# A stacked graph kernel: the first pair of batches split into two halves, and PSUM banks given out as asked for

## The chip, the cores and the metric

The kernel runs on one core of one Trainium2 chip. The time is the device time of one execution in microseconds (us), the median of several runs. A profiled execution is one more run, with every instruction recorded. The engines are named PE (TensorE matmul), PEld (TensorE weight load, which overlaps PE), DVE (VectorE), ACT (ScalarE), POOL (GpSimd) and SP (SyncE, which issues transfers here).

## The reference, cut to what matters

The input x has 64 batches of 256 nodes with 128 features, in float32; adj is a 256x256 matrix shared by all batches. Four layers follow one another, each on a layer norm with a ReLU and each added to x:

```python
h = relu(layernorm(x)); x = x + gated(h, adj)     # five recurrent steps, each: m = adj @ h for each batch,
                                                  # r, z = sigmoid gates of m and h, hv = tanh(W5 m + U5 (r*h)),
                                                  # h = (1 - z) * h + z * hv
h = relu(layernorm(x)); x = x + relu([h, A'h, A'A'h ...] @ Theta + bias)
h = relu(layernorm(x)); y = (adj @ h + h) @ W + bias; x = x + y / max(norm(y), 1e-12)
h = relu(layernorm(x))
pre[b,i,j,:] = W1 h[b,i] + W2 h[b,j] + b_lin      # 256 features for each of 256 x 256 pairs of nodes
e[b,i,j] = sum over features of a * leaky_relu(pre) + adj[i,j]
x = x + sigmoid(softmax_j(e) @ h)
```

The last layer's scores e are most of the work: 64 x 256 x 256 pairs of nodes with 256 features each.

## The kernel before

**Tiling.** The 64 batches are taken two at a time: 32 pairs, and a feature-by-node tile of a pair is 128 partitions x 512 columns (2 batches x 256 nodes). For each pair, `front(p)` computes the first three layers and the operands of the scores; then 64 slots of score work follow, 32 for each of two blocks of 128 rows i (`ic`); then `tail(p, ic, ...)` makes the softmax and the output of one block.

**A front.** It is a Python generator that yields where it must wait: `yield ENGINE, since, bank, gate`. A recurrent step is a chain over engines: PE mixes nodes (`mix_nodes`), ACT copies the result out (mT), PE projects (u3t, w4t), ACT takes the tanh for r, DVE makes rh, PE projects (w34, w5t, u5t), ACT takes two tanhs, three elementwise passes follow on DVE (for pairs after the first, one of them, d, is on POOL), PE turns the result to token order (`to_token`) and ACT copies it out (h). After the fifth step come x1, a norm, two mixes and three products (x2), a norm, a mix, a product and a norm of rows (x3), a last norm, and four projections: s2a and s2c, s2n, s1b, s1a. A small matmul, `quarter`, and a trip through DRAM (`row`, `rows`) give two more operands that only a tail reads.

**A score tile.** A slot n stands for four rows i (32 apart) of both batches, and has two halves (k = 0 and 1) of 128 features. One tile is 128 x 4 x 2 x 256. `work_on_tile` makes it: DVE with one instruction (k = 0, from s1a and s2a in PSUM), ACT with 16 small ones (k = 1, from s1b and s2p in PSUM), POOL with 8 small ones (either). For three slots in ten, POOL issues a DMA that adds one half onto the other (`add_pair`). `score` then lets PE sum over features with four matmuls of 512 columns into the block's bank. 13 buffers (`tiles`) hold score tiles.

**Order.** There is no scheduler at run time. A planner in the program keeps a clock for each engine with estimated durations, and always lets the engine that is least far choose: tails first, then fronts in the order of their keys (constants for the first pairs are chains too, keys -1 and NPAIR), then score tiles. `in_order` fixes each engine's program to the order in which it was chosen. At the beginning the fronts of pairs 0 and 1 are begun together; one more is begun for each pair scored. A front p with 0 < p < NPAIR is held to a due time while a bank is spare (`chain_ready`: `due = STEPS_OF_FRONT * (scored / 128 - (p - 2)) / SPREAD`, with SPREAD 1.7). The constants must be complete ("all" in `SET_UP`) before a front may start its second layer.

**PSUM.** Eight tiles of 128x512, `banks`, are dealt out by hand: two for s2a (`s2v`, by the parity of p), one for s2p, two for the scores (`pes`, by the parity of the block), and three in a list `spare` that fronts and tails take from and give back to. While no score is made yet, pair 0's front uses the banks of s2p and the scores for its r, pr and pv.

```python
s2v = banks[:2]
s2p = banks[2].rearrange("p (b n) -> p b n", b=NB)
pes = banks[3:5]
...
spare = [[b, 0.0] for b in banks[5:]]
```

Of the kernel before, what the change touches and what calls it, by code (L numbers as in the profile page):

```python
# [31 lines left out]
def kernel(  # L32
# [63 lines left out]
    s2v = banks[:2]  # L96
    s2p = banks[2].rearrange("p (b n) -> p b n", b=NB)
    pes = banks[3:5]
# [19 lines left out]
    spare = [[b, 0.0] for b in banks[5:]]  # L118
# [6 lines left out]
    def by_feature(b):  # L125
        return b.rearrange("p (b n) -> p b n", b=NB)

    def by_token(b):
        return b.rearrange("p (b c n) -> p b c n", b=NB, c=NC)
# [262 lines left out]
    def inverse_root(t, of, *scaled):  # L392

        nc.gpsimd.tensor_scalar(t, of, scaled[0], scaled[2], op0=scaled[1], op1=scaled[3])
        nc.gpsimd.tensor_tensor(t, t, minus_half, op=OP.pow)  # L395
# [9 lines left out]
    def project(pp, w, t, start=True, stop=True):  # L405

        side_by_side(pp, w, flat(t), start, stop)

    def mix_nodes(pm, h, a):

        pm = by_feature(pm)
        for b in range(NB):
            for c in range(NC):
                side_by_side(pm[:, b, :], h[:, b, c, :], a[:, c, :], c == 0, c == NC - 1)

    def to_feature(pt, h):

        pt = by_token(pt)
        for b in range(NB):
            for c in range(NC):  # L420
                nc.tensor.transpose(pt[:, b, c, :], h[:, b, c, 0:D], ident)

    def to_token(pt, ht):

        pt = by_token(pt)
        for b in range(NB):
            for c in range(NC):
                nc.tensor.transpose(pt[:, b, c, :], ht[:, b, c * P:(c + 1) * P], ident)  # L428

    def project_token(pp, pairs):  # L430

        pp = by_token(pp)
        for b in range(NB):
# [16 lines left out]
    PROJECT, MIX, TURN, PRODUCT, PRODUCTS = 0.86, 1.74, 0.80, 0.88, 2.64  # L450
    COPY, BIASED, TANH, ELEMENTS = 0.48, 0.58, 0.57, 0.61

    def norm(src, since, h):

        stats = work.tile([P, NB * NC, 3], F32, name="stats")
        mv = work.tile([P, NB * NC, 2], F32, name="mv")
        s, h = rows_of(src), rows_of(h)[:, :, 0:D]
        yield DVE, since
        for k in range(0, NB * NC, 2):
            nc.vector.bn_stats(stats[:, k:k + 2, :].rearrange("p k s -> p (k s)"), s[:, k:k + 2, :].rearrange("p k d -> p d k"))  # L460
        t = ran(DVE, 0.8, since)
# [7 lines left out]
        for k in range(NB * NC):  # L469
            nc.scalar.activation(h[:, k, :], s[:, k, :], AF.Relu, bias=mv[:, k, 0:1], scale=mv[:, k, 1:2])  # L470
        return ran(ACT, 1.55, t)

    def copied(name, bank, t):

        c = feat(name, **(SHORT if name not in KEPT else KEPT[name]))
        nc.scalar.copy(c, by_feature(bank[0]))  # L476
        t = ran(ACT, COPY, t)
        spare.append([bank[0], t])
        return c, t

    KEPT = {"hT": dict(bufs=4), "hT3": {}, "s2n": {}}

    READY = {}

    def front(p):
# [4 lines left out]
        x0 = XIN.pop(p)  # L490


        h = tok("h", **SHORT)
# [5 lines left out]
        t = ran(PE, TURN, t, b[1])  # L499
        yield ACT, t  # L500
        hT, t_hT = copied("hT", b, t)
        for step in range(STEPS):
# [3 lines left out]
            t = ran(PE, MIX, t_h, b[1])  # L506
            yield ACT, t
            mT, t_m = copied("mT", b, t)
            if p == 0:
                pr, r, pv = ([banks[k], 0.0] for k in (3, 2, 4))  # L510
                yield PE, t_hT, 0, lambda: "first" in SET_UP
                project(pr[0], u3t, hT, stop=False)
                ran(PE, PROJECT, t_hT)
                yield PE, t_m
                project(pr[0], w4t, mT, start=False)
                t = ran(PE, PROJECT, t_m)
                project(pv[0], w5t, mT, stop=False)
                ran(PE, PROJECT)
                yield ACT, t
            else:  # L520
# [4 lines left out]
                t = ran(PE, 2 * PROJECT, t_m, t_hT, pr[1])  # L525
                yield ACT, t, 1
                r = take()
            nc.scalar.activation(r[0], pr[0], AF.Tanh, bias=br, scale=0.5)  # L528
            t = ran(ACT, TANH, t, r[1])
            yield DVE, t  # L530
            rh = feat("rh", **SHORT)
            nc.vector.scalar_tensor_tensor(rh, by_feature(r[0]), 1.0, hT, op0=OP.add, op1=OP.mult)  # L532
            t_rh = ran(DVE, ELEMENTS, t)
            if p == 0:
                yield PE, t
                project(pr[0], w34, mT, start=False)
                t_z = ran(PE, PROJECT, t)
                yield PE, t_rh
                project(pv[0], u5t, rh, start=False)
                t = ran(PE, PROJECT, t_rh)  # L540
            else:
                spare.append([r[0], t_rh])
                yield PE, t_rh, 1
                project(pr[0], w34, mT, start=False)
                t_z = ran(PE, PROJECT, t)
# [3 lines left out]
                t = ran(PE, 2 * PROJECT, t_rh, pv[1])  # L549
            yield ACT, t_z  # L550
            nc.scalar.activation(pr[0], pr[0], AF.Tanh, bias=bz, scale=0.5)  # L551
            t_z = ran(ACT, TANH, t_z)
            yield ACT, t

            d = feat("d", **SHORT)
            if p < 1:
                nc.scalar.activation(pv[0], pv[0], AF.Tanh, bias=bh, scale=1.0)
                t = ran(ACT, TANH, t)
                yield DVE, t
                nc.vector.tensor_sub(d, by_feature(pv[0]), hT)  # L560
                t = ran(DVE, ELEMENTS, t)
            else:
                nc.scalar.activation(d, by_feature(pv[0]), AF.Tanh, bias=bh, scale=1.0)  # L563
                t = ran(ACT, TANH, t)
# [5 lines left out]
            nc.vector.scalar_tensor_tensor(by_feature(pr[0]), by_feature(pr[0]), 1.0, d, op0=OP.add, op1=OP.mult)  # L570
            t = ran(DVE, ELEMENTS, t, t_z)
            yield DVE, t
            hT_new = feat("hT", bufs=4)
            nc.vector.scalar_tensor_tensor(hT_new, by_feature(pr[0]), 0.5, hT, op0=OP.mult, op1=OP.add)  # L574
            hT = hT_new
            t_hT = ran(DVE, ELEMENTS)
            if p > 0:
                spare.append([pr[0], t_hT])
# [3 lines left out]
            t = ran(PE, TURN, t_hT, b[1])  # L582
            if step < STEPS - 1:
                yield ACT, t
                h = tok("h", **SHORT)
                nc.scalar.copy(h, by_token(b[0]))  # L586
                t_h = ran(ACT, COPY, t)
                spare.append([b[0], t_h])
        yield DVE, t
        x1 = tok("x1", tag="x12", bufs=3)  # L590
        nc.vector.tensor_add(x1, x0, by_token(b[0]))
        t = ran(DVE, ELEMENTS, t)
# [3 lines left out]
        h = tok("h", **SHORT)  # L596
# [4 lines left out]
        t = ran(PE, MIX, t_h, b[1])  # L601
# [5 lines left out]
        t = ran(PE, TURN, t_h, b[1])  # L607
        yield ACT, t
        hT, t = copied("hT", b, t)
# [3 lines left out]
        t = ran(PE, MIX, t_h, b[1])  # L613
# [5 lines left out]
        t = ran(PE, PRODUCTS, t, po[1])  # L619
        yield DVE, t  # L620
        pt = rows_of(by_token(po[0]))
        nc.vector.tensor_add(pt, pt, bias1.unsqueeze(1).to_broadcast([P, NB * NC, D]))
        t = ran(DVE, ELEMENTS, t)
        yield DVE, t
        x2 = tok("x2", tag="x12", bufs=3)
        nc.vector.scalar_tensor_tensor(x2, by_token(po[0]), 0.0, x1, op0=OP.max, op1=OP.add)
        t = ran(DVE, ELEMENTS)
# [3 lines left out]
        h = tok("h", **SHORT)  # L631
# [4 lines left out]
        t = ran(PE, MIX, t, b[1])  # L636
# [5 lines left out]
        t = ran(PE, PRODUCT, t, po[1])  # L642
        yield DVE, t
        pt = rows_of(by_token(po[0]))
        nc.vector.tensor_add(pt, pt, bias2.unsqueeze(1).to_broadcast([P, NB * NC, D]))
        t = ran(DVE, ELEMENTS, t)
        yield ACT, t
        sq = tok("sq", **SHORT)
        nc.scalar.square(sq, by_token(po[0]))
        t = ran(ACT, COPY, t)  # L650
        yield DVE, t
        rn = work.tile([P, NB * NC], F32, name="rn")
        nc.vector.tensor_reduce(rn, rows_of(sq), AX.X, OP.add)
        t = ran(DVE, ELEMENTS, t)
# [5 lines left out]
        x3 = tok("x3")  # L660
        for k in range(NB * NC):
            nc.vector.scalar_tensor_tensor(rows_of(x3)[:, k], pt[:, k], rn[:, k:k + 1], rows_of(x2)[:, k],
                                           op0=OP.mult, op1=OP.add)
        t = ran(DVE, 1.04, t)
# [3 lines left out]
        h3 = work.tile([P, NB, NC, D + 1], F32, name="h3")  # L668
# [5 lines left out]
        t = ran(PE, TURN, t, b[1])  # L674
        yield ACT, t
        hT, t_hT = copied("hT3", b, t)
        s2a = s2v[p % 2]
        yield PE, max(t_hT, t_s2v[p % 2])
        project(s2a, w2n[:, 0:P], hT)
        t_s2a = ran(PE, PROJECT, t_hT, t_s2v[p % 2])  # L680
        yield ACT, t_s2a
        s2c = feat("s2c")
        nc.scalar.copy(s2c, by_feature(s2a))
        t_s2a = ran(ACT, COPY, t_s2a)
        yield PE, t_hT, 1
        b = take()
        tokens = flat(hT).rearrange("p (q g i) -> p q g i", g=4, i=32)
        for g in range(4):
            nc.tensor.matmul(b[0][g * 32:(g + 1) * 32, 0:P], g2, tokens[:, :, g, :], start=True, stop=True, skip_group_check=True)
        t = ran(PE, 0.35, t_hT, b[1])  # L690
        yield ACT, t
        quarter = work.tile([P, P], F32, name="quarter", bufs=1)
        nc.scalar.copy(quarter, b[0][:, 0:P])
        t = ran(ACT, 0.3, t)
        spare.append([b[0], t])
        yield DVE, t
        turned = work.tile([P, P], F32, name="turned", bufs=1)
        nc.vector.transpose(turned, quarter)
        s1o = work.tile([P, NB * NC], F32, name="s1o")
        nc.vector.tensor_scalar(s1o, turned[:, 2:P:32], b_odd, None, op0=OP.add)  # L700
        ran(DVE, 0.4, t)
        row = dram.tile([2, NB * N], F32, name="row", bufs=2)
        for k in range(2):
            nc.sync.dma_start(row[k].rearrange("(q g i) -> g q i", g=4, i=32), quarter[k:P:32, :].rearrange("g (q i) -> g q i", i=32))
            t = moved(t) if k else max(t, moved(t) - 2.2)
        rows = work.tile([P, 2, NB, N], F32, name="rows")
        nc.sync.dma_start(rows.rearrange("p k b n -> p (k b n)"), row.rearrange("k t -> (k t)").unsqueeze(0).to_broadcast([P, 2 * NB * N]))
        lin, s2o = rows[:, 0], rows[:, 1]
# [5 lines left out]
        t = ran(PE, PROJECT, t_hT, b[1])  # L714
        yield ACT, t
        s2n, t_2 = copied("s2n", b, t)
# [343 lines left out]
```

## Time and profile before

| | |
|---|---|
| median of 3 runs | 4939.74 us (4939.73 to 4947.85) |
| the profiled execution | 4942.53 us, span of its instructions 4940.7 us |
| PE, DVE, ACT, POOL busy | 96%, 95%, 94%, 94% of the span |
| granted TensorE clock, mean | 0.995 of full |
| large score tiles | 1817 on DVE, 231 + 785 on POOL, 1263 on ACT |
| DMA adds of one half onto the other | 614, of 1024 KB each, 7.9 us to landing |

A line of the timeline gives the start and the duration in us, the engine, the line of the kernel, the operation, the tile written and the tiles read with their shapes, and how many in a row; in brackets, how long the engine was idle before and what released it. A line of the busy time by stretch gives the stretch, its length, then for PE, PEld, DVE, ACT and POOL the busy us and the number of instructions, then the granted clock, the busy share of the DMA engines and GB/s. A line of the waits gives who waited for whom, the us in total, how often, and the longest.

### The profile page before, as it was taken

The page shows a single profiled execution, that of the slowest core. Times are in us where ns is not written, and L with a number is a line of the kernel's source. Part 1 is how long each engine was busy: PE and PEld are TensorE (multiplying, and loading weights), DVE is VectorE, ACT ScalarE, POOL GpSimd, SP SyncE. Part 2 cuts the span into 40 slices and gives each one's busy share as a digit, 9 for nine tenths or more (in the row PEclk, how much of TensorE's full clock was granted, in tenths as well). Part 3 has the DMA queues.
Part 4 walks back from the last instruction along what each step waited for, and adds up shares of the span by engine and source line. Part 5 has one row for each costly group of instructions (what it writes and reads, how often), then busy time and mean ns, then how long its engine had stood idle before and what let it go on. Part 6 is the DMA issues. An engine that isn't in the chain of part 4 may idle for free. (4 is left out here: it accounts for less than half of the span.)

```text
span 4940.7 us, 133662 instructions
## 1 busy us (share of the span) xinstructions
PE 4758.5 (96%) x52231; PEld 1739.0 (35%) x52231; DVE 4682.1 (95%) x3358; ACT 4644.4 (94%) x12121; POOL 4659.6 (94%) x9446
## 2 busy tenths in 40 slices
PE   8999999999999999999999999999999999999987
PEld 3333333333333333333333333333334333333322
DVE  3999999999999999999999999999999999999998
ACT  3999999999999999999999999999999999999998
POOL 1999999999999999999999999999999999999998
PEclk9999999999999999999999999999999999999999
DMA  0577677677666676766677676767666766766677
GB/s 18 121 144 146 142 147 144 135 144 147 140 142 138 141 155 143 145 139 139 140 146 145 139 145 130 155 139 146 134 137 141 151 137 140 146 141 141 142 158 148
DMA packets 133132, 687.42 MB, mean 139 GB/s; under 512 B 15121, under 2 KB 49809, under 8 KB 53905
## 3 DMA queue, kind: packets, MB, share of 16 engines
q0 software_dynamic: 88416, 643.86, 65.1%
q1 hardware_dynamic: 43360, 35.01, 2.3%
q8 instruction: 408, 6.68, 0.5%
q14 instruction: 228, 1.86, 0.1%
q10 hardware_dynamic: 720, 0.00, 0.0%
HBM read 26.48 MB, written 8.52 MB: 7 GB/s over the span
## 5 line engine op out<-in xcount | busy, mean ns | idle before, releaser
L873 ACT ACTIVATE rl<-bank,s1b 128x256 f32<-128x256 f32 x10104 | 4050.2, 793 | 128.9 <-DMA rl<-rl 70.9
L859 DVE TENSOR_TENSOR rl<-s1a,bank 128x2048 f32<-128x2048 f32 x1817 | 4064.8, 2280 | 90.4 <-DMA rl<-rl 62.7
L881 POOL TENSOR_SCALAR rl<-s2n,s1b 128x256 f32<-128x256 f32 x6280 | 2951.1, 656 | 64.2 <-DMA rl<-rl 28.2
L940 PE MATMUL bank<-rl,win_n 128*32 128x512 f32 x17752 | 2191.5, 594 | 57.1 <-DVE rl L859 28.9
L940 PE MATMUL bank<-rl,win 128*32 128x512 f32 x10104 | 1316.5, 594 | 0.0
L940 PEld LDWEIGHTS bank<-rl,win_n 128*32 128x32 f32 x17752 | 559.4, 110 | 1216.5 <-issue 992.8
L881 POOL TENSOR_SCALAR rl<-s2c,s1a 128x256 f32<-128x256 f32 x1848 | 872.7, 637 | 5.9 <-DMA rl<-rl 1.2
L898 POOL DMA_DIRECT2D rl<-rl x614 | 569.9, 940 | 22.2 <-DVE rl L859 10.8
L940 PEld LDWEIGHTS bank<-rl,win 128*32 128x32 f32 x10104 | 323.1, 110 | 641.4 <-issue 533.1
L400 PE MATMUL bank<-mT,wts 128*32 128x512 f32 x2560 | 336.6, 597 | 6.5 <-ACT mT L476 4.9
L400 PE MATMUL bank<-adj_t,h 128*32 128x256 f32 x5120 | 310.6, 383 | 13.7 <-ACT h L586 13.4
L567 POOL TENSOR_TENSOR d<-d,hT 128x512 f32<-128x512 f32 x155 | 230.4, 1486 | 71.3 <-ACT d L563 71.2
L400 PEld LDWEIGHTS bank<-adj_t,h 128*32 128x32 f32 x5120 | 164.0, 111 | 191.2 <-issue 51.1
L470 ACT ACTIVATE h<-x,mv 128x128 f32<-128x128 f32 x384 | 177.7, 699 | 10.6 <-DVE mv L466 9.7
L428 PE MATMUL bank<-ident,hT 128*128 128x128 f32 x640 | 105.4, 288 | 69.2 <-DVE hT L574 61.7
L400 PE MATMUL bank<-hT,wts 128*32 128x512 f32 x1280 | 168.7, 597 | 0.0
L400 PE MATMUL bank<-mT,w 128*32 128x512 f32 x1280 | 167.4, 593 | 0.8 <-ACT bank L528 0.8
L400 PE MATMUL bank<-rh,u5t 128*32 128x512 f32 x1280 | 167.3, 592 | 0.7 <-DVE rh L532 0.7
L528 ACT ACTIVATE bank<-bank,gate_b 128x512 f32<-128x512 f32 x160 | 144.3, 902 | 20.5 <-PE bank L400 16.5
L476 ACT COPY mT<-bank 128x512 f32<-128x512 f32 x160 | 139.3, 871 | 24.1 <-PE bank L400 20.0
L551 ACT ACTIVATE bank<-bank,gate_b 128x512 f32<-128x512 f32 x160 | 151.4, 946 | 11.3 <-PE bank L400 11.3
L563 ACT ACTIVATE d<-bank,gate_b 128x512 f32<-128x512 f32 x155 | 150.0, 967 | 7.4 <-PE bank L400 7.4
(167 smaller groups left out, 3382.2 us busy)
## 6 DMA issues: line engine op xcount, KB each, us to landing
rl<-rl POOLq DMA_DIRECT2D x614, 1024.0 KB, 7.9
rows<-row SPq DMA_DIRECT2D x32, 512.0 KB
xin<-in_x_dram SPq DMA_DIRECT2D x64, 128.0 KB
out_dram<-o SPq DMA_DIRECT2D x64, 128.0 KB
row<-quarter SPq DMA_DIRECT2D x64, 2.0 KB
w_raw<-in_L_gnn_w_w_dram SPq DMA_DIRECT2D x3, 128.0 KB
th_raw<-in_L_gnn_Theta_dram SPq DMA_DIRECT2D x1, 320.0 KB
adj_n<-in_adj_dram SPq DMA_DIRECT2D x1, 256.0 KB
```

The source lines that it names most:

```text
L400: nc.tensor.matmul(o[g:g + 32], w[:, g:g + 32], t, start=start, stop=stop, skip_group_check=True)
L470: nc.scalar.activation(h[:, k, :], s[:, k, :], AF.Relu, bias=mv[:, k, 0:1], scale=mv[:, k, 1:2])
L476: nc.scalar.copy(c, by_feature(bank[0]))
L528: nc.scalar.activation(r[0], pr[0], AF.Tanh, bias=br, scale=0.5)
L551: nc.scalar.activation(pr[0], pr[0], AF.Tanh, bias=bz, scale=0.5)
L563: nc.scalar.activation(d, by_feature(pv[0]), AF.Tanh, bias=bh, scale=1.0)
L567: nc.gpsimd.tensor_sub(d, d, hT)
L859: nc.vector.tensor_tensor(t, rows.to_broadcast(whole), ops["s2a"].unsqueeze(1).to_broadcast(whole), op=OP.min)
L873: nc.scalar.activation(t[:, g, b, :], s2p[:, b, :], AF.Relu, bias=ops["s1"][1][:, b, i:i + 1], scale=-1.0)
L881: nc.gpsimd.tensor_scalar(t[:, part, b, :], ops["s2n" if k else "s2c"][:, b, :], ops["s1"][min(k, 1)][:, b, row], MOST_NEGATIVE, op0=OP.mi ...
L898: nc.gpsimd.dma_start(out=t.rearrange("p g b n -> p (g b n)"), in_=z.rearrange("p g b n -> p (g b n)"), accum_op=OP.add)
L940: nc.tensor.matmul(pe[g * 32:(g + 1) * 32, :], w[:, 31 - r:63 - r], flat(t[:, g]), start=False, stop=(left[block] == 0), skip_group_check= ...
```

## The change

The helpers of a front (`mix_nodes`, `to_feature`, `to_token`, `project_token`, `norm`) and the planner's estimates take the number of batches, one or two, instead of always two. `front(p, batches)` is begun twice for the first pair, with one batch each, under keys 0 and 0.5; both are `alone`. Such a front works on 256 columns; its tiles of the moment are pieces of two score tiles each (`lent`), which go back to `tiles` at its end, and its lasting tiles (`kept`) are halves of tiles shared by both. An `alone` front keeps the order of operations that pair 0 had, with d on DVE.

For the first pair a block of scores is now one batch with all its 256 rows instead of 128 rows of both batches, so that a slot stands for eight rows of one batch. A block of the first batch can begin when that batch's front is through.

All eight banks are in `spare`. The first front to need it takes one for s2p and keeps it; s2a takes one at the end of its front and gives it back when its last tile is begun; a block of scores takes one with its first tile and gives it back when its tail has read it; at most two blocks are open at once.

The diff, cut to its core:

```diff
-    s2v = banks[:2]
-    s2p = banks[2].rearrange("p (b n) -> p b n", b=NB)
-    pes = banks[3:5]
...
-    spare = [[b, 0.0] for b in banks[5:]]
+    spare = [[b, 0.0] for b in banks]
...
-    COPY, BIASED, TANH, ELEMENTS = 0.48, 0.58, 0.57, 0.61
+    COPY, BIASED, TANH, ELEMENTS = (None, 0.32, 0.48), (None, 0.40, 0.58), (None, 0.40, 0.57), (None, 0.36, 0.61)
...
-    def front(p):
+    def front(p, batches):
...
+        nb = len(batches)
+        alone = nb < NB
+        own = slice(batches[0], batches[-1] + 1)
+        x0 = (XIN[p] if alone else XIN.pop(p))[:, own]
+        lent, piece = [], [0]
+        if alone:
+            lent = [tiles.pop() for _ in range(2)]
+            halves = [t[0][:, g, b, :] for t in lent for g in range(4) for b in range(NB)]
...
-            if p == 0:
-                pr, r, pv = ([banks[k], 0.0] for k in (3, 2, 4))
-                yield PE, t_hT, 0, lambda: "first" in SET_UP
+            if alone:
+                yield PE, t_hT, 1, lambda: "first" in SET_UP
+                pr = take()
                 project(pr[0], u3t, hT, stop=False)
...
-        s2a = s2v[p % 2]
-        yield PE, max(t_hT, t_s2v[p % 2])
-        project(s2a, w2n[:, 0:P], hT)
+        yield PE, t_hT, 1
+        s2a = take()
+        project(s2a[0], w2n[:, 0:P], hT)
...
+        if alone:
+            yield ACT, t_2, not S2P
+            if not S2P:
+                S2P.append(take())
+            s2p.append(by_feature(S2P[0][0])[:, own])
+            nc.scalar.copy(s2p[0], s2n)
...
+        for u in batches:
+            READY[p, u] = ops
+        tiles.extend([t, max(t_b, t_n, t_lin)] for t, _ in lent)
+
+    def across(u):
+
+        return [(0, c) if READY[u]["alone"] else (c, u[1]) for c in range(NB)]
...
+        used = banks_of.pop(u)
+        spare.append([used, t])
...
     def where(n):
-        return n // SLOTS, n % SLOTS // 32, n % 32
+        return (n // SLOTS, n % SLOTS // 32), n % 32
...
+        if k == 0 and not ops["left"] and ops["bank"][0] is not None:
+            spare.append(list(ops["bank"]))
+            ops["bank"][0] = None
...
-            if block not in left:
-                if block >= 2 and block - 2 not in t_pe:
+            if u not in left:
+                if len(banks_of) == 2 or not spare:
                     continue
-                since = max(since, t_pe.get(block - 2, 0.0))
+                since = max(since, min(b[1] for b in spare))
...
-        begin(p, front(p))
+            begin(p, front(p, tuple(range(NB))))
+        else:
+            for b in range(NB):
+                begin(p + b / NB, front(p, (b,)))
...
-        if not isinstance(key, tuple) and 0 < key < NPAIR and spare:
+        if not isinstance(key, tuple) and 1 <= key < NPAIR and spare:
```

## The prediction

> **What bounds the kernel now.** I read the page's busy times first, then the busy time by stretch, then the timeline of the opening, then the waits. Page and stretches (us, then PE, PEld, DVE, ACT, POOL busy, granted clock, DMA):
>
> ```profile
> PE 4758.5 (96%) x52231; PEld 1739.0 (35%) x52231; DVE 4682.1 (95%) x3358; ACT 4644.4 (94%) x12121; POOL 4659.6 (94%) x9446
> ...
> 0.00:132.00 132.00, 109.10 (x1107) 47.79 (x1107) 43.47 (x120) 46.98 (x83) 15.64 (x28) 0.88 0.07 20
> 132.00:4800.00 4668.00, 4544.01 (x50156) 1659.55 (x50152) 4517.66 (x3171) 4475.04 (x11706) 4526.96 (x9179) 1.00 0.70 142
> ```
>
> From 132 us on, four engines are each busy for 96 to 97% and none can be named as the bound alone. In the 132 us before, DVE stands idle for 88.5, ACT for 85.0 and POOL for 116.4: no score tile can be made until the first pair's front is through. The timeline of the opening shows its two halves, and a slow clock:
>
> ```profile
> 91.93 0.69 DVE L591 TENSOR_TENSOR x<-xin,bank 128x512 f32<-128x512 f32 x1 [1.27 <-PE bank L428]
> 132.04 4.49 DVE L859 TENSOR_TENSOR rl<-s1a,bank 128x2048 f32<-128x2048 f32 x2 [4.14 <-ACT s1a L732]
> ...
> 20.00:25.00 5.00, 2.95 (x24) 1.64 (x28) 2.84 (x12) 1.90 (x5) 1.29 (x2) 0.61 0.00 0
> 25.00:30.00 5.00, 5.00 (x38) 3.06 (x34) 0.79 (x5) 0.92 (x2) 0.00 (x0) 0.50 0.00 0
> 30.00:35.00 5.00, 5.00 (x28) 1.26 (x18) 3.99 (x22) 0.66 (x1) 0.00 (x0) 0.52 0.01 2
> ```
>
> Five recurrent steps take until 91.93, the three layers after them another 40.1. The front of the second pair runs beside it: POOL's d (L567) ends for its fifth time at 119.5. In the steady part the longest waits of the tile makers are for a buffer that a DMA add gives back:
>
> ```profile
> ACT rl L873 <- DMA rl<-rl: 70.9, 43, 5.2
> DVE rl L859 <- DMA rl<-rl: 62.1, 53, 3.5
> ```
>
> No wait there names a PSUM bank that is short; but the order is planned, so a shortage would show as an earlier choice, not as a wait.
>
> **What the Trainium skill says.** "VectorE: DVE Perf Modes", section on the TRN2 errata: VectorE and ScalarE pay a fixed cost per instruction, TensorE does not. The trace agrees: DVE takes 0.69 us for 512 columns and 0.42 for 256 (L277), an ACT copy 0.58 for 512 and 0.27 for 128 (L693), while four 32-column matmuls take 0.86 for 512 columns and, in L400's mix, 0.43 for 256. "TensorE: Matmul & The Clock Gate", section "What's actually happening": an array that was not busy runs at half its clock. The stretches above (0.50) and 0.50 for 120 to 130 us agree. "PSUM — Partial Sum Buffer", "Specifications (TRN2)": eight banks of 2 KiB a partition; a 128x512 tile here fills one, so eight is all there is to give out.
>
> **The change part by part.**
>
> *Half batches.* The first pair's front becomes two, each of 256 columns. By the rows above a half costs DVE 0.42, an ACT copy 0.37 and tanh 0.45 (on the line between 128 and 512 columns), PE half. One recurrent step as a chain, before: mix 1.75, mT 0.58, w4 0.86, tanh 0.66, rh 0.69, u5 0.86, tanh 0.66, three DVE passes 2.08, turn 0.58, copy 0.59: 9.3, and some 2.2 for eleven hand-overs of about 0.2: 11.5. Half: 0.87 + 0.37 + 0.43 + 0.45 + 0.42 + 0.43 + 0.45 + 1.26 + 0.29 + 0.37 = 5.3, plus 2.2: 7.5. The trace's steps took 14.2, 22.4, 15.5, 15.5 and 15.3, mix to mix, since PE also serves the second pair and the constants, part of it at half clock. So PE's list counts too. In the changed order PE has 43.6 us of work (0.86 for four matmuls of 512, 0.145 a transpose, 0.5 and 0.22 for those of the constants) before the first batch's fifth step is turned, against 62.6 before. Following the first batch through that list, instruction by instruction with these durations and the half clock left where it is, its mixes start at 7.0, 16.6, 28.8, 41.8 and 52.4, and x1 is there at 60. The three layers halve less, as POOL's power (1.0 to 1.05 on 4 columns) and the hand-overs stay: norms 4.7 to 3.4 each, products 2.64 to 1.33, four projections 3.4 to 1.7; along the list 34 instead of 40.1. That gives 94; I add 5 for seams that such a walk misses: **first tile at about 99 instead of 132**. Bounds: 92 (no seams), and 115, where PE loses as much time as before.
>
> *What was cover in the opening.* At 132 PE had done 89.5 us of listed work; at the new first tile 73.4. Left for later are two of the second pair's five steps (2 x 6.85, less a turn) and the second batch's last layer and projections (3.5). They now run beside full engines. So each engine's gain is its idle time saved, less work added:
> - PE: 132 - 89.5 = 42.5 lost before, 99 - 73.4 = 25.6 after: 17. Nothing added.
> - DVE: busy 43.5 - 2.8 (four passes of the second pair) - 3.9 (second batch's rest) + 3.8 (halves done) = 40.6; idle 58.4 against 88.5 saves 30; added in all 25 x 0.15 + 0.9 = 4.7: 25.
> - ACT: 47.0 - 5.7 (nine) - 4.7 + 6 = 42.6; idle 56.4 against 85.0 saves 28.6; added 41 x 0.17 = 7: 22.
> - POOL: 15.6 - two d's 2.5 + three inverse roots 3.8 = 16.9; idle 82.1 against 116.4 saves 34; added five roots x 1.25 = 6.2: 28.
>
> The four must move together; PE can lag, as from 4800 to 4900 us it was only about 82% busy. I take **20**, between PE's 17 and the mean of 23.
>
> *Instructions that stay.* The counts of large tiles are the same: 1817 on DVE, 614 DMA adds; 16 of ACT's 10104 small ones go to POOL. A tile of the first pair reads columns of the same number, so I cost it at nothing.
>
> *Queues.* SP gets two more row writes and one more broadcast (0.5 and 0.35 to issue). The load of the third pair's x waits in SP for the second batch's x1, with the first batch's rows behind it; that x1 precedes those rows by some 15 us of PE's list, and the rows are read only by a tail, some 75 us on. Nothing. Two relu tiles are lent to each half front; when tiling starts two of 13 are still out. For about 15 us; nothing to 3, I take 0.
>
> *Banks.* Fixed before: two for s2a, one for s2p, two for scores, three to share. Now one is fixed for s2p, and at a change of pairs two s2a and two scores leave three, otherwise four or five. The trace shows no price of a shortage: worth between +10 (a tenth of the roughly 130 us that each engine idles in the steady part) and -15 (below, as a rival); I take 0 and keep both ends.
>
> **The rivals.**
> 1. *Forecast: the start moves, half is given back.* 55%. 4939.7 - 20 = 4920.
> 2. *PE is the start's bound.* The list, not the chain, sets it: PE loses its 42.5 us again, first tile at 115. Then PE gains nothing, the others some 6 to 12: about 4936 with 4 for the mean. For: PE was busy 109 of 132. Against: the walk shows PE waiting less with two chains. 15%. That the change doesn't do what it says is this case.
> 3. *The order after the start is worse.* A front that has a spare bank is held to its due time (chain_ready tests `spare`). With three to share, this was often lifted; with four or five it is nearly always on, so front steps come late and in a burst at the change of pairs, and PE serves score tiles later: makers wait for buffers. Price: each 1 us a pair on the makers is 31 us; from 0.65 the gain is gone, from 1.0 it is slower: at 1.2 us, 4940 - 20 + 37 = 4957. For: makers already wait 62 to 71 us on buffers. Against: fronts have 1.7 pairs of time and nothing shows them late. 10%.
> 4. *Banks help as well.* The same pool lets a step start when it is due: 10 to 20 off, 4902. 20%.
>
> **How the numbers follow.** The profiled execution took 4942.5 around a span of 4940.7; the median of three is 4939.7, 2.8 less. The sums are differences, so I take them from the median: 4920. Less than 0.2% (9.9 us) can't be told from no change. Cases 1 and 4 give 75%, of which about 2 fall under 9.9 when the first tile is near 108 or re-planning costs 0.3 us a pair; half of case 2's misses add 3: faster 0.76, same 0.15, slower 0.09. Range: case 4 below, case 2 above, and part of case 3: 4899 to 4940.
>
> **What would show it.** The first large DVE tile at 92 to 108 us; x1 of the first batch near 60; DVE rows of 256 columns at 0.42; about 56 us of DVE idle before the first tile; front steps of the second pair inside the first scores. In the steady part 76 DVE tiles in 200 us as before. Wrong if: the first tile comes after 115, the half passes cost over 0.5, or DVE makes under 75.5 tiles in 200 us.

## The result, and the profile after

The changed kernel takes **4924.27 us** (median of five runs, 4923.45 to 4935.50); the kernel before, in five runs on the same chip, 4944.86 us (4939.73 to 4947.85). The ratio is 0.9967, with a 95% interval of 0.9952 to 0.9981: 16 us less, between 9 and 24 (the two medians lie 20.6 apart). Forecast were 20 less and 4920 us. The profiled execution of the changed kernel took 4930.46 us around a span of 4928.2 us, against 4942.53 and 4940.7 before.

Busy time of the page, and busy time by stretch (us, then busy us and instructions of PE, PEld, DVE, ACT and POOL, granted clock, DMA share, GB/s), changed kernel:

```profile
PE 4768.4 (97%) x52471; PEld 1739.2 (35%) x52471; DVE 4713.3 (96%) x3389; ACT 4643.9 (94%) x12142; POOL 4670.5 (95%) x9473
```

```profile
0.00:92.00 92.00, 82.10 (x1105) 42.61 (x1106) 43.12 (x139) 43.43 (x101) 12.91 (x30) 0.96 0.10 25
20.00:25.00 5.00, 5.00 (x86) 3.29 (x82) 3.22 (x11) 2.34 (x6) 1.21 (x2) 1.00 0.02 5
25.00:30.00 5.00, 4.23 (x55) 2.12 (x58) 4.56 (x25) 3.65 (x9) 0.00 (x0) 1.00 0.00 0
30.00:35.00 5.00, 5.00 (x90) 2.66 (x86) 1.49 (x8) 2.51 (x6) 0.00 (x0) 1.00 0.02 3
```

PE does in 92 us about as many instructions (1105) as it did before in 132 (1107). The three stretches from 20 to 35 us, where the clock before was 0.61, 0.50 and 0.52, now have it at 1.00: two chains keep PE busy where one left gaps (from 20 to 25 us PE was busy for 2.95 of 5). Up to the first large tile, PE stood at half clock for 30.7 us before and for 6.8 now. In the runs below it is 20.4 to 27.3 us where the first pair has one front (e2, e11, e12), and 3.4 to 6.9 where it has two (all the others).

The timeline of the opening (start and duration in us, engine, line, operation, tiles):

```profile
54.37 0.42 DVE L628 TENSOR_TENSOR rl<-xin,bank 128x256 f32<-128x256 f32 x1 [0.65 <-PE bank L428]
...
90.26 0.69 DVE L608 SCALAR_TENSOR_TENSOR bank<-bank,d 128x512 f32<-128x512 f32 x1
90.86 0.42 DVE L463 BATCH_NORM_STATS2 stats<-rl 128x6 f32<-128x256 f32 x1
91.19 0.67 DVE L612 SCALAR_TENSOR_TENSOR hT<-bank,hT 128x512 f32<-128x512 f32 x1
91.78 2.28 DVE L934 TENSOR_TENSOR rl<-s1a,bank 128x2048 f32<-128x2048 f32 x1
```

```profile
90.42 0.46 ACT L785 ACTIVATE s1a<-bank,blin_s 128x256 f32<-128x256 f32 x1
90.78 1.20 ACT L946 ACTIVATE rl<-bank,s1b 128x256 f32<-128x256 f32 x3
```

x1 of the first batch is there at 54.4 us (before: 91.9, for both batches), and DVE's first large tile starts at 91.8 (before: 132.0). Just ahead of it DVE still does half-sized work of the second batch (256 columns) and the third step of the second pair (L608 and L612, 512 columns): two of that pair's five steps are left over, as the order foretold.

So tiling starts 40 us earlier, and yet the whole is only 16 us shorter. Two kinds of loss stand between: work that was done under the opening and is now done later, and something in the steady part. The waits from 300 to 4600 us (who waited for whom: us in total, times, longest) don't show the second:

```profile
ACT rl L946 <- DMA rl<-rl: 61.3, 42, 3.7
DVE rl L934 <- DMA rl<-rl: 53.2, 42, 3.3
```

They are a little shorter than before in the same stretch:

```profile
ACT rl L873 <- DMA rl<-rl: 68.6, 42, 5.2
DVE rl L859 <- DMA rl<-rl: 60.1, 52, 3.5
```

But the changed kernel makes 1612 large DVE tiles in that stretch and the kernel before 1621. To see where the time goes, progress was counted: the time at which k thirty-seconds of the 27856 score matmuls (L1010, before L940) have begun, less that of the kernel before, each from one profiled execution. One thirty-second is the work of one pair, so k = 1 stands for "after the first pair". A negative number is a lead; single points wander by 2 to 3 us. (In the kernel before, k = 1, 2, 5, 16 and 28 are reached at 286.1, 438.1, 888.0, 2541.0 and 4358.8 us.)

| kernel (of the experiments below) | k=1 | 2 | 5 | 16 | 28 |
|---|---|---|---|---|---|
| changed | -28.7 | -30.5 | -17.3 | -7.0 | -13.2 |
| changed, again (e1) | -28.8 | -29.7 | -17.3 | -2.9 | -9.6 |
| banks alone (e2) | -6.8 | -4.5 | -3.0 | +3.2 | +4.3 |
| halves, three banks (e3) | -28.8 | -30.2 | -30.6 | -27.9 | -31.9 |
| changed, two steps left out (e4) | -42.8 | -40.7 | -35.8 | -28.2 | -38.4 |
| changed, SPREAD 1.75 (e5) | -26.7 | -28.9 | -24.3 | -19.5 | -26.2 |
| e3 with SPREAD 1.75 (e6) | -27.3 | -29.0 | -26.9 | -18.4 | -36.4 |
| due time lifted (e7) | -29.3 | -30.4 | -31.0 | -37.0 | -40.1 |
| three banks, due time kept (e8) | -25.0 | -30.4 | -25.9 | -21.2 | -20.5 |
| e7 with SPREAD 1.75 (e9) | -26.7 | -28.4 | -26.8 | -22.0 | -25.2 |
| changed, AHEAD 10 (e10) | -26.1 | -30.4 | -21.0 | +2.0 | +9.6 |
| before, SPREAD 1.75 (e11) | -0.1 | +1.2 | +6.4 | +26.5 | +36.9 |
| before, two steps left out (e12) | -9.9 | -2.6 | +3.1 | +6.8 | +5.5 |

Of 40 us, 29 are left after the first pair, 30 after the second, and 17 after the fifth; later the lead is 7 and 13. Every kernel with two half fronts that makes all its steps leads by 28 to 31 us after two pairs, whatever its order; none with one front leads by more than 5.

### The profile page after: what moved, and what is told of

It reads as the page before. It is cut to its first block, busy times and chain, and to the rows that moved or that the text cites. A ratio compares the mean times of both kernels' runs of the same rounds, so it can differ in the third digit from the quotient of the medians.

```text
span 4928.2 us, 134012 instructions
## 1 busy us (share of the span) xinstructions
PE 4768.4 (97%) x52471; PEld 1739.2 (35%) x52471; DVE 4713.3 (96%) x3389; ACT 4643.9 (94%) x12142; POOL 4670.5 (95%) x9473
## 4 chain that ended last, share of the span: by engine, by line
PE 31%; POOL 18%; DVE 12%; DMA 7%; ACT 6%; issue 4%; POOLq 0%; ACTq 0%; DVEq 0%
PE bank L1010 19%; POOL rl L951 14%; PE bank L397 11%; DVE rl L934 10%; DMA rl<-rl 7%; ACT rl L946 5%; POOL rl L971 2%; POOL d L605 1%; PE bank L428 1%; POOL mv L392 1%; DVE mv L469 0%; DVE hT L612 0%; PE bank L420 0%; DVE bank L608 0%; POOL sc L818 0%
## 5 line engine op out<-in xcount | busy, mean ns | idle before, releaser
L951 POOL TENSOR_SCALAR rl<-s2n,s1b 128x256 f32<-128x256 f32 x6296 | 2966.0, 668 | 50.6 <-DMA rl<-rl 19.2
L1010 PE MATMUL bank<-rl,win_n 128*32 128x512 f32 x17768 | 2211.3, 596 | 56.0 <-DVE rl L934 28.0
L1010 PE MATMUL bank<-rl,win 128*32 128x512 f32 x10088 | 1321.9, 597 | 0.0
L1010 PEld LDWEIGHTS bank<-rl,win_n 128*32 128x32 f32 x17768 | 557.2, 110 | 1215.1 <-issue 981.7
L951 POOL TENSOR_SCALAR rl<-s2c,s1a 128x256 f32<-128x256 f32 x1848 | 874.8, 643 | 7.1 <-DMA rl<-rl 2.5
L1010 PEld LDWEIGHTS bank<-rl,win 128*32 128x32 f32 x10088 | 323.4, 110 | 655.5 <-issue 532.1
L397 PE MATMUL bank<-mT,wts 128*32 128x512 f32 x2480 | 326.2, 594 | 1.6 <-ACT mT L521 1.3
L397 PE MATMUL bank<-adj_t,h 128*32 128x256 f32 x4960 | 300.5, 381 | 7.5 <-ACT h L623 6.4
L473 ACT ACTIVATE h<-x,mv 128x128 f32<-128x128 f32 x376 | 176.2, 720 | 13.5 <-DVE mv L469 13.2
L565 ACT ACTIVATE bank<-bank,gate_b 128x512 f32<-128x512 f32 (+1 forms) x165 | 148.5, 900 | 19.4 <-PE bank L397 14.3
L588 ACT ACTIVATE bank<-bank,gate_b 128x512 f32<-128x512 f32 (+1 forms) x165 | 154.0, 934 | 9.5 <-PE bank L397 9.4
L521 ACT COPY mT<-bank 128x512 f32<-128x512 f32 x155 | 137.1, 885 | 26.8 <-PE bank L397 24.8
L428 PE MATMUL bank<-ident,hT 128*128 128x128 f32 x620 | 101.7, 287 | 57.4 <-DVE hT L612 54.4
```

What stands on the lines that cost most here:

```text
L397: nc.tensor.matmul(o[g:g + 32], w[:, g:g + 32], t, start=start, stop=stop, skip_group_check=True)
L565: nc.scalar.activation(seen(r), seen(pr), AF.Tanh, bias=br, scale=0.5)
L588: nc.scalar.activation(seen(pr), seen(pr), AF.Tanh, bias=bz, scale=0.5)
L951: nc.gpsimd.tensor_scalar(t[:, part, b, :], other(ops["s2n" if k else "s2c"], b), rows[:, part, b], MOST_NEGATIVE, op0=OP.min, op1=OP.max)
L1010: nc.tensor.matmul(pe[g * 32:(g + 1) * 32, :], w[:, 31 - r:63 - r], flat(t[:, g]), start=False, stop=(left[u] == 0), skip_group_check=True)
```

## The experiments

### The changed kernel once more, and its parts: e1 to e4

**e1, changed kernel again,** no edit. Is the fall of the lead between the second and the fifth pair chance, or a property of the order?

> The changed kernel once more, beside the three that follow. Start theory (the halves bring the first tile from 132 to 92 us, about half of that is given back while the work left for later is made up): 15 to 22 us under the kernel before. Its first profile showed a lead of 40 us at the first tile, 25 after one pair, 10 after five and 12.5 at the end, while the medians of the two kernels stand 16 to 20 apart. If the loss between the second and the fifth pair is a property of the order, the lead in this profile falls again to about 10 by the fifth pair; if it was that one execution's, the lead stays near 20 to 25.

Measured: 4926.19 us, ratio 0.9963 (0.9950 to 0.9976). The first large DVE tile starts at 92.0; the lead is 29.7 after the second pair and 17.3 after the fifth. The fall belongs to the order.

**e2, banks alone.** The pool of eight banks stays; the first pair is one whole front again, in the order of operations that it had.

```diff
+        early = p == 0
...
-            if alone:
+            if early:
...
-            for b in range(NB):
-                begin(p + b / NB, front(p, (b,)))
+            begin(p, front(p, tuple(range(NB))))
```

> All eight banks are given out as asked for, but the first pair has one front of 512 columns, in the order of operations that it had before. Start theory: first tile at 125 to 132 us, total within 8 us of the kernel before. Banks theory (a good part of the gain is from the pool: front steps start when due): 8 to 20 us under the kernel before, with the first tile still at about 130.

Measured: 4938.09 us, ratio 0.9989 (0.9982 to 0.9995), 2 to 9 us less by the interval. The timeline has the first large DVE tile 4 us earlier than before:

```profile
127.81 2.29 DVE L935 TENSOR_TENSOR rl<-s1a,bank 128x2048 f32<-128x2048 f32 x1 [2.94 <-ACT s1a L786]
```

These 4 us needn't be the banks'. e11 (below) gives out no bank differently, and up to its first large tile PE, DVE and ACT run the same instructions in the same order as in the kernel before; yet that tile comes 4.5 us earlier. Its first tile, and the stretch from 20 to 35 us in the kernel before and then in e11:

```profile
127.57 2.29 DVE L859 TENSOR_TENSOR rl<-s1a,bank 128x2048 f32<-128x2048 f32 x1 [2.51 <-ACT s1a L732]
```

```profile
20.00:35.00 15.00, 12.95 (x74) 5.95 (x74) 7.62 (x38) 3.48 (x7) 1.29 (x2) 0.54 0.00 1
20.00:35.00 15.00, 12.62 (x98) 6.27 (x102) 7.90 (x38) 4.07 (x8) 1.29 (x2) 0.66 0.00 1
```

With more clock PE gets further through the same list (98 instructions against 74). Up to the first tile it stands at half clock for 30.7 us before, 20.4 in e11 and 20.5 in e2. So the clock alone can move this start by as much as e2 moves it, and what the banks add to the start isn't shown.

The start, then, comes from the halves: 36 of the 40 us or more. Nothing of e2's lead lasts (3.0 after the fifth pair, none at the sixteenth), but its profiled execution was the slowest of its 22, so its later columns say little.

**e3, halves with three banks.** The halves stay. Once the second half is ready, fronts and tails together may hold no more than three banks, as before, and the test of the due time asks whether one of these three is free, not whether any bank is spare. The two banks for s2a (asked for with 2, counted in held_s2a) stay outside the three, as do s2p's and the two of the scores.

```diff
+    def free_to_take(bank=1):
+        if (0, 1) not in READY or bank == 2:
+            return bool(spare)
+        in_use = 8 - len(spare) - len(banks_of) - len(S2P) - held_s2a[0]
+        return bool(spare) and in_use < 3
...
-        if engine != e or bank and not spare or gate and not gate():
+        if engine != e or bank and not free_to_take(bank) or gate and not gate():
...
-        if not isinstance(key, tuple) and 1 <= key < NPAIR and spare:
+        if not isinstance(key, tuple) and 1 <= key < NPAIR and free_to_take():
```

> Two half fronts for the first pair; from the end of the second one on, fronts and tails together may hold at most three banks, as before the change, while s2a, s2p and the scores keep their own. Start theory: first tile at 92 us as in the changed kernel, and 12 to 22 us under the kernel before. Banks theory: first tile at 92 us, but only 0 to 8 us under the kernel before.

Measured: **4894.71 us**, ratio 0.9899 (0.9883 to 0.9915): 50 us less than before, the fastest of all the kernels here, and outside both expectations. Its first tile is at 90.6 and its lead after two pairs is 30.2, as in the changed kernel; but it keeps it, 30.6 after five. The 13 us that part it from e1 and from the changed kernel by then don't come from the halves, which are the same. What differs is the order, and which bank a step takes.

**e4, two steps left out of the changed kernel.** The front of the second pair makes three recurrent steps instead of five: just the two that are left over when tiling starts.

```diff
+        steps = STEPS - 2 if p == 1 else STEPS
-        for step in range(STEPS):
+        for step in range(steps):
```

> The changed kernel with the second pair's front making three recurrent steps instead of five (this leaves out computation: the second pair's result is another one). These two steps are what the shorter opening no longer covers: on PE 2 x 6.85 = 13.7 us, on ACT ten passes of 0.63 = 6.3, on DVE six of 0.69 = 4.1, on POOL two of 1.4 = 2.8. Theory that this work is what takes the lead from 40 down: 5 to 13 us under the changed kernel, and the lead after the first pair nearer 33 than 25. Rival (the work left over runs in gaps of the score phase at no price, and the lead is lost elsewhere): within 4 us of the changed kernel.

Measured: 4908.94 us, ratio 0.9934 (0.9921 to 0.9947), 15 us under the changed kernel and 17 under e1; 5 to 13 were expected. After the first pair the lead is 42.8 instead of 28.7 and 28.8: the two steps are worth 14 us, and with them gone the whole of the 40 us that the first tile moved is still there. PE's time for them in the prediction was 2 x 6.85 = 13.7. **This is the first loss, shown:** two steps that lay under the old opening now cost about their time on PE, under full engines.

**e12, the same two steps left out of the kernel before.** There they lie under the opening.

> The kernel before with the second pair's front making three recurrent steps instead of five (this leaves out computation: the second pair's result is another one). There the opening covers these steps. Cover theory: first tile within 6 us of 132, lead after the first pair 0 to 5 us, against the 13 to 15 that the same omission gave in the changed kernel. Rival (the two steps cost the same wherever they stand): lead of 13 to 15.

Measured: 4955.05 us, ratio 1.0021 (1.0014 to 1.0028), 10 us more. The first tile doesn't move:

```profile
132.07 2.29 DVE L860 TENSOR_TENSOR rl<-s1a,bank 128x2048 f32<-128x2048 f32 x1 [3.20 <-ACT s1a L733]
```

So nothing that leads to the first tile waited for these steps. Whether they cost nothing there, the run doesn't say. The lead after the first pair is 9.9 us, between the two expectations (0 to 5, and 13 to 15); over the first half of the second pair it is 14 on average, and at its end 2.6. The room that the steps left was filled at once: x1 of the second pair comes at 90.2 us here, and came at 147.3 in the kernel before,

```profile
90.18 0.67 DVE L592 TENSOR_TENSOR x<-xin,bank 128x512 f32<-128x512 f32 x1
```

```profile
147.32 0.68 DVE L591 TENSOR_TENSOR x<-xin,bank 128x512 f32<-128x512 f32 x1
```

and by 132 us PE has begun 1187 instructions instead of 1107. Later work of the same front moved under the opening, so the omission took away more than the two steps' own place. That the run as a whole is longer with work left out says something else, taken up next: the planner chose another order for the rest, and that one is worse.

### Where the rest goes: e5 to e11

The planner decides with whatever spare banks and due times it sees, so each edit gives another order over 4.8 ms. e5, e6, e9 and e11 measure what another order costs when nothing else is meant: SPREAD goes from 1.7 to 1.75, which lets fronts come 3% later. e7 and e8 take the two halves of e3's edit apart.

**e5, changed kernel; e6, halves with three banks; e11, the kernel before; each with**

```diff
-    STEPS_OF_FRONT, SPREAD, AHEAD = 109, 1.7, 2
+    STEPS_OF_FRONT, SPREAD, AHEAD = 109, 1.75, 2
```

> The changed kernel with the fronts' pace constant SPREAD at 1.75 instead of 1.7: no instruction added or taken away, only another order from the second pair on. The changed kernel loses about 15 us of its lead between the second and the fifth pair in both of its profiles. Order theory (any other order draws another amount of idle time in the steady part, some 10 to 20 us either way): anywhere from 4900 to 4945, and the lead need not fall there. Bank theory (with seven banks in the pool the score phase is worse than with three): within 8 us of 4925, the lead again falling to about 10.

> The halves with the cap of three banks for fronts and tails, SPREAD at 1.75. Order theory: anywhere from 4885 to 4930. Bank theory (the cap itself is what brought 4895): within 8 us of 4895.

> The kernel before with SPREAD 1.75, again only another order. Order theory: 5 to 20 us away from the kernel before, to either side. If the kernel before is not sensitive to it: within 5 us. The lead at the end of the first pair within 4 us of zero either way.

**e7, due time lifted:** of e3's three edits only the last (a front isn't held to its due time when three or more banks are in use); no limit on banks. **e9** is e7 with SPREAD 1.75. **e8, limit of three kept, due time strict:** e3 without its last edit.

> The changed kernel's banks without a cap, but the due time of a front is not asked for while fronts and tails hold three banks or more, as it was before the change whenever the list of three was empty. Pacing theory (the due time that now always holds makes front steps come late): 4890 to 4900, as with the cap. Cap theory (what helps is that fewer banks are in use): about 4925. Order theory: anywhere between.

> Due time lifted while fronts and tails hold three banks or more, with SPREAD 1.75. So far the halves with a strict due time stand at 4916 to 4926 (three orders), with the lifted one at 4895, 4907 and 4912. Pacing theory: 4895 to 4912 again. Order theory (the three lifted ones were three good draws): anywhere from 4895 to 4930.

> The cap of three banks for fronts and tails, but the due time holds whenever any bank of the eight is free. Pacing theory: about 4925, as in the changed kernel. Cap theory: 4890 to 4900. Order theory: anywhere between.

**e10, changed kernel with AHEAD 10:** a front may be ten of its 109 steps ahead of its due time, instead of two.

> The changed kernel, its strict due time kept, but a front may be ten steps ahead of it instead of two. Pacing theory, in the form that fronts are held back for too long: 4895 to 4912. If what helps is only that a front which holds banks is let through when they are short, this loosening does nothing: 4916 to 4930. Order theory: anywhere between.

Measured (us, and ratio to the kernel before with its interval):

| | SPREAD 1.7 | SPREAD 1.75 |
|---|---|---|
| before | 4944.86 | e11: 4979.60, 1.0063 (1.0048 to 1.0078) |
| changed: due time strict, no limit | 4924.27 | e5: 4923.96, 0.9964 (0.9951 to 0.9977) |
| strict, limit of three | e8: 4916.54, 0.9950 (0.9933 to 0.9966) | not run |
| lifted, no limit | e7: 4906.97, 0.9930 (0.9914 to 0.9946) | e9: 4922.65, 0.9948 (0.9933 to 0.9963) |
| lifted, limit of three (e3) | 4894.71, 0.9899 (0.9883 to 0.9915) | e6: 4911.70, 0.9944 (0.9926 to 0.9963) |
| changed, AHEAD 10 | e10: 4960.53, 1.0025 (1.0012 to 1.0037) | not run |

What follows:

- **An order by itself is worth tens of microseconds.** SPREAD alone moves the medians of the kernel before by +35, of e3 by +17, of e7 by +16 (by the ratios 9, with intervals that overlap), of the changed kernel by 0. Any single difference of this size between two of these kernels may be no more than a new draw. The shifts of e10 and e11 are larger than any that was expected; e6, e7, e8 and e9 fell where only "another order" put them.
- **Lifting the due time** gives 17 us at SPREAD 1.7 without the limit and 22 with it, but 1 at 1.75. Letting fronts run ahead in another way (e10) costs 36. The third rival's mechanism, fronts that come late since their due time is nearly always on, isn't there: counted in score matmuls, a front stands at the same place with the due time strict or lifted. Its last s1a is done 0.26 of a pair's matmuls ahead of its own pair in the kernel before, in the changed one, in e3 and in e7; its x1 comes 0.90, 0.89, 0.90 and 0.90 ahead (means over pairs 5 to 30). What moves it is SPREAD 1.75 (0.21) and AHEAD 10 (0.39), and e10, where fronts come earliest, is the slowest kernel with halves.
- **The limit of three** is faster than no limit in all three pairs (by the medians: e3 against e7 12, e8 against the changed kernel 8, e6 against e9 11; by the ratios 15, 8 and 2). One sign three times, each less than a change of SPREAD can make: a hint that more banks to share are no help, not a finding.
- **The halves** are faster than the kernel before in all of the seven orders without AHEAD 10, by 16 to 50 us. With SPREAD 1.75 on both sides (e5 and e11) the medians lie 56 us apart.

Why the changed kernel loses its 12 to 13 us between the second and the fifth pair can be located, if not explained. The stretch from 300 to 1000 us, changed kernel and then e3:

```profile
300.00:1000.00 700.00, 678.33 (x7420) 244.69 (x7412) 678.78 (x471) 656.86 (x1718) 671.54 (x1364) 0.99 0.68 139
```

```profile
300.00:1000.00 700.00, 688.11 (x7540) 248.97 (x7536) 677.70 (x479) 670.52 (x1748) 686.30 (x1386) 1.00 0.70 143
```

PE, ACT and POOL are each busy 10 to 15 us less in the changed kernel. DVE is busy for the same time, but with eight instructions fewer. The groups of DVE in that stretch (busy us, mean ns; then idle before), changed kernel and then e3, say which:

```profile
L934 DVE TENSOR_TENSOR rl<-s1a,bank 128x2048 f32<-128x2048 f32 x260 | 581.8, 2276 | 15.5 <-DMA rl<-rl 7.2 <-PE bank L1010 6.8 <-ACT rl L946 1.6
L469 DVE SCALAR_TENSOR_TENSOR mv<-stats,mv 128x4 f32<-128x4 f32 x18 | 15.8, 876 | 0.9 <-POOL mv L392 0.8
...
L741 DVE TENSOR_SCALAR s1o<-turned,odd_one 128x4 f32<-128x4 f32 x5 | 3.8, 755 | 0.2
```

```profile
L943 DVE TENSOR_TENSOR rl<-s1a,bank 128x2048 f32<-128x2048 f32 x266 | 595.2, 2276 | 14.0 <-DMA rl<-rl 6.7 <-PE bank L1020 5.7 <-POOL rl L960 1.5
L477 DVE SCALAR_TENSOR_TENSOR mv<-stats,mv 128x4 f32<-128x4 f32 x18 | 5.0, 277 | 3.2 <-POOL mv L400 3.2
...
L750 DVE TENSOR_SCALAR s1o<-turned,odd_one 128x4 f32<-128x4 f32 x5 | 1.4, 289 | 0.2
```

Six large tiles fewer are 13.4 us of DVE. They are made up by two tiny instructions on four columns: mv takes 15.8 us instead of 5.0, s1o 3.8 instead of 1.4, together 13.2 more. Half of it is a single one. The timeline of the changed kernel:

```profile
419.59 6.49 DVE L469 SCALAR_TENSOR_TENSOR mv<-stats,mv 128x4 f32<-128x4 f32 x1
...
420.21 1.48 POOL L818 TENSOR_TENSOR sc<-sc,rows 128x512 f32<-128x512 f32 x1
...
421.47 2.83 POOL L951 TENSOR_SCALAR rl<-s2n,s1b 128x256 f32<-128x256 f32 x6
424.15 2.75 POOL L951 TENSOR_SCALAR rl<-s2c,s1a 128x256 f32<-128x256 f32 x6
426.00 2.27 DVE L934 TENSOR_TENSOR rl<-s1a,bank 128x2048 f32<-128x2048 f32 x1
426.11 1.65 ACT L473 ACTIVATE h<-xin,mv 128x128 f32<-128x128 f32 x4 [4.92 <-DVE mv L469]
...
428.33 1.94 PE L1010 MATMUL bank<-rl,win_n 128*32 128x512 f32 x8 [6.09 <-DVE rl L934]
```

and its busy time in that stretch:

```profile
420.00:430.00 10.00, 3.91 (x28) 0.96 (x30) 10.00 (x5) 5.08 (x15) 6.91 (x15) 0.74 0.53 107
```

An instruction whose median is 0.17 us stands for 6.5 while POOL runs one operation after another; DVE counts as busy, ACT waits 4.92 us for mv and PE 6.09 for the tile behind it. In e1 the same mv stands for 6.54 us at 421.14. In e3 it falls at another moment, and the same ten microseconds have PE at 10.00 and ACT at 9.93.

The Trainium skill has the likely reason, which no run here isolates. "SBUF — State Buffer", section "Who interferes with whom": VectorE and GpSimd share one pair of ports, under an exclusive lock, and a VectorE instruction with two inputs in SBUF blocks against a GpSimd instruction that reads SBUF. mv reads stats and mv, both in SBUF; for s1o the same section lists `tensor_scalar` among the operations that can take the pair. The large tiles have one input in PSUM, and never stretch (2257 to 2289 ns in this stretch). The trace agrees with that division: in the whole of the changed kernel's trace, mv and s1o are the only groups of more than 15 DVE instructions in which one takes over 1.1 times the group's median. (In the kernel before there is one more, once: L570, 1.54 us instead of 0.69, with an input in PSUM.) But the wait is longer than one instruction of POOL (about 0.47 us each for L951, 1.48 for L818 in the rows above). If it was the lock, it was lost to about a dozen instructions in a row.

That this costs the changed kernel its lead is an account of one stretch, not a tested cause: no run put mv elsewhere, or its inputs in PSUM. From 300 to 1000 us mv and s1o together take 19.6 us in the changed kernel and 15.2 in e1, which lose 12 to 13 us of lead between the second and the fifth pair, and 5.3 to 11.6 in e3 and e5 to e10, which lose 0 to 9; but 23.8 in e11, which loses 5. From 300 to 4600 us they take 53.8 in e7, 58.0 in e3, 66.1 in e8, 69.8 in e6, 76.3 in e9, 77.3 in the changed kernel and 94.7 in e5, which goes roughly with their times, and 50.6 before against 124.4 in e11. Against it stand e10, the slowest of the halves with only 72.5, and e1: the changed kernel's own order, with 64.5 in a profiled execution that took 5 us longer. What makes e10 slow, and what else makes one order better than another, stays open.

## Why the prediction was right, point by point

**The forecast was the first case** (the start moves, half is given back): 20 us forecast, 16 measured (9 to 24). Its parts were less right than their sum.

- **Durations of the halves** held: DVE's passes took 0.42, ACT's copies 0.37, its tanh 0.45, as read off the rows of before. POOL's inverse root was costed at 1.25 on two columns; its power took 0.70 and the step before it 0.19, so 0.9.
- **The walk to x1** gave mixes at 7.0, 16.6, 28.8, 41.8 and 52.4 and x1 at 60. They came at 6.95, 17.9, 28.4, 37.6 and 47.0, and x1 at 54.4. The step that failed is "the half clock left where it is": from 20 to 35 us the clock is 1.00. Most of the 5.6 us, 3.8, comes between the third and the fourth mix, where the walk still had half clock (up to 34.8 us in the kernel before); how the rest divides isn't shown. The prediction cited the Trainium skill, "TensorE: Matmul & The Clock Gate", "What's actually happening", for an array at half its clock when it isn't busy, and then didn't apply it to the change, which keeps it busy. Nor is a half clock read off one trace a fixed part of a start: e11, with PE's old list, had 20.4 us of it instead of 30.7.
- **From x1 to the first tile** 34 were listed and 5 allowed for seams; measured 37.4. So the first tile came at 91.8, not 99: 5.6 us from x1 and 1.6 from the seams, and 0.2 us below the lower bound of 92. (That bound is given as "no seams"; the prediction's own sum without seams is 94.)
- **The ledger of the opening.** With the first tile at 91.8 and the same working, PE gains 42.5 - (91.8 - 73.4) = 24 us, and DVE, ACT and POOL more (their idle time before the first tile fell from 88.5, 85.0 and 116.4 to 48.7, 48.4 and 78.9). With the prediction's own terms for added work that is 35, 30 and 31 for these three, and 30 for the mean of the four. The lead after the first two pairs was 29 to 30: between PE's number and the mean, as the rule of the prediction had it, and near the mean. What was off is the term that went in, the first tile. That the steps left over cost about PE's time for them is what e4 showed.
- **"Instructions that stay" and "Queues: nothing"** are not contradicted: e3 has both and keeps its lead.
- **Banks: 0, with +10 and -15 as ends.** The pool alone gave 5 us (2 to 9), and its 4 at the start may be the clock's. The fourth rival (banks help by 10 to 20 more) isn't seen. But the ends came from a tenth of the idle time, and a different order alone moves these kernels by up to 35: the term stood for the new order as a whole, and its ends were too narrow for that.
- **The second rival** (PE is the bound of the start, first tile at 115) is out with a first tile at 91.8.
- **The third rival** (the order after the start is worse) did happen in kind, at about half its price of 37: the changed kernel and e1 give back 12 to 13 us between the second and the fifth pair, and 17 and 20 by the twenty-eighth. Its mechanism did not: fronts come no later than before.
- **The test named in advance** for the steady part was 76 large DVE tiles in 200 us, and under 75.5 as wrong. From 300 to 1000 us the changed kernel makes 260, or 74.3, against 268, or 76.6, before. By its own test the prediction fails there. From 300 to 4600 it is 1612 against 1621, 75.0 and 75.4: the mark of 75.5 was too high, since the kernel before misses it as well.

So the number came out near by luck: two errors stood against each other. The start gave about 10 us more than the 20 taken, and the order, costed at nothing, then took back more than that. Another order with the same halves ends anywhere from 4895 (e3) to 4960 us (e10).

## What to carry to other kernels

A chain that leaves its engine idle can pay twice, in the gap and in the clock after it (half clock for 20 to 31 us of these openings with one chain, for 3 to 7 with two). Split it in two that interleave, and cost the halves at the clock of the busy engine, not the one that the trace of before shows. What the old gap covered has then to be paid among busy engines (14 us here, about its time on PE): list it before adding up the gain. Where a planner fixes the order, measure how far a change that means nothing moves the time, before giving any difference of that size a cause.

## What the runs showed that was not expected

An instruction of four columns can hold VectorE for microseconds. Over the whole run, before and then changed, and s1o in e11 (groups by shape; busy us, mean ns):

```profile
L466 DVE SCALAR_TENSOR_TENSOR mv<-stats,mv 128x4 f32<-128x4 f32 x128 | 38.8, 303 | 26.2 <-POOL mv L395 25.7
```

```profile
L469 DVE SCALAR_TENSOR_TENSOR mv<-stats,mv 128x4 f32<-128x4 f32 x124 | 61.1, 493 | 13.4 <-POOL mv L392 12.7
```

```profile
L700 DVE TENSOR_SCALAR s1o<-turned,odd_one 128x4 f32<-128x4 f32 x32 | 86.7, 2708 | 1.1
```

Their undisturbed times are 0.17 and 0.23 us, mv's longest 7.3 before and 6.6 changed, s1o's longest in e11 9.5. Such a row hides in a page: DVE is "busy", its group is far down the list, and the waits name DVE. It shows as a group whose mean is several times the duration of its shape.
